# A base product over eight batches at once, with quarters of 512 tokens, in an adapter and LoRA-mixture kernel

## The chip, the cores and the metric

The kernel runs on one core of a Trainium2 chip. The metric is the time of one execution in microseconds as the device reports it, the median of three runs. One further execution was taken with the hardware profiler. TensorE (PE) multiplies matrices and writes to the accumulator memory PSUM, VectorE (DVE) and ScalarE (ACT) work elementwise, and SyncE's queue (SP) issues nearly all transfers. Each engine takes its instructions strictly in the order in which the program lists them, and waits at an instruction until the semaphores that it names have been reached.

## The reference

There are 8 batches of 256 tokens with 1024 features, all in float32. Each batch picks one of eight 1024 x 1024 matrices; its result goes through a base layer with bias, and through a mixture of eight rank-16 LoRA experts whose weights come from a router.

```python
y = einsum('bsi,boi->bso', x, weight[adapter_ids])
base_out = einsum('btd,od->bto', y, base_W) + base_b
probs = softmax(einsum('btd,nd->btn', y, router_W) + router_b)   # 15 outputs
topk_p, topk_i = top_k(probs, 8)
w = einsum('btk,btke->bte', topk_p, onehot(expert_map[topk_i]))
h = einsum('btd,erd->bter', y, A)
lora = einsum('bter,eor->bto', h * w[..., None], B) * 2.0
return x + base_out + lora
```

## The kernel before, in words

**Adapter stage** (lines 284 to 439). One pass of the loop at line 370 handles one batch. It multiplies with seven half-size products in place of eight (Winograd's form): 512 x 512 pieces of the adapter matrix times pieces of x that are 128 tokens wide, in the blocks of `block` (line 238), 16 matmuls each. The results go to `ys[0]` (batches 0 to 3) and `ys[1]` (batches 4 to 7). `project` (line 98) multiplies the batch's y with the stacked A and router matrices into the PSUM tile `ph`; ACT copies the 128 columns of h out of it (line 115), DVE adds the router bias to the other 15 (line 116, tile `lg`), and `weigh` makes the expert weights and the product `hw`. `turn` (line 199) transposes `hw` on PE into `pt` and ACT copies it to `hwTs`. Beside this work `prepare` (line 261) builds, a piece per batch, the seven left operands of the base product, and stores them to a scratch tensor in HBM.

The last batch ends so: blocks for a21, s4 and a22 on PE, then `turn` of batch 6 (line 442), then `project` of batch 7 (line 443). In the DVE queue there stand the add that completes y of batch 7 (line 423), the four differences (`differences`, line 175; instructions on line 186) of the first base product, the eight sums and differences of `prepare(7)` (lines 269 to 276), and then `lg` of batch 7 and its `weigh`.

**Base stage** (lines 449 to 705). It is Winograd's form twice. The outer level has seven products of 512 x 512 pieces of the base matrix and runs once for each of two groups `g` of four batches; each outer product is again seven inner blocks (`product`, line 496). An inner block has four matmuls, stationary 128 x 128 and moving 128 x 256 tokens (`block`, line 474), and in four of seven outer products two more for the LoRA term (line 487). In the trace each float32 matmul is two records. PSUM holds `pa`, `pb` and `pc`, each 2 KB a partition and twice, beside `pe` (line 540) and `pt`. The blocks of one product are, in order, a11 (pa), s1 (pc), s2 (pa), a12 (pb), s3 (pa), s4 (pc), a22 (pa). The value that stands in `pa` is read out (`take`, `plus`) before the next block adds to it, so each block on `pa` waits for the read of the `pa` block before it.

Between the blocks stand the gaps (`gap`, line 530): each puts two waiting DVE steps from the queues `soon` and `later` ahead of the next read. Such steps are differences of inner operands (line 186), outer sums (line 630), and results plus residual x (line 601) with their store. `load_left` (line 163) fetches the left operand of a product, 1 MB and 0.75 MB, two products ahead, once for each group. The last product of all (`split`) has one half of its result in `pe`, so that the first half is added and stored while PE makes the second.

The pools of the base stage are opened after those of the adapter stage are closed (line 449), and lie over the same memory.

Of the kernel before, what the change touches and what calls it, by code (L numbers as in the profile page):

```python
# [28 lines left out]
def kernel(  # L29
# [4 lines left out]
    xr: bass.AP,  # L34
    ids: bass.AP,
# [25 lines left out]
    assert ER == P and E == 8 and B % GB == 0  # L61
# [4 lines left out]

    tpool = ctx.enter_context(tc.tile_pool(name="t", bufs=6))
    ps_t = ctx.enter_context(
        tc.tile_pool(name="ps_t", bufs=1, space=bass.MemoryType.PSUM)
    )  # L70
# [27 lines left out]
    def project(b, ar_sb, rpool, ps_h, order=(0, 1)):  # L98
# [6 lines left out]
        for j in order:  # L105
            for k in range(KC):
                nc.tensor.matmul(  # L107
                    ph[:, j],
                    lhsT=y[:, k // KH, th, k % KH // 2, bi, k % 2, ts(j, P)],
                    rhs=ar_sb[:, k, :],  # L110
                    start=(j == order[0] and k == 0),
                    stop=(k == KC - 1),
                    skip_group_check=True,
                )
# [59 lines left out]

    def differences(right):

        b11, b12, b21, b22 = right[:, 0, 0], right[:, 0, 1], right[:, 1, 0], right[:, 1, 1]
        t = {}

        def minus(n, of, less):  # L180
            def run():
                t[n] = tpool.tile([P, 2 * S], F32, name="tt").rearrange(
                    "p (k o) -> p k o", k=2
                )
                x, y = (t[v] if isinstance(v, int) else v for v in (of, less))
                nc.vector.tensor_sub(t[n], x, y)  # L186
                return t[n]

            return run

        return [minus(1, b12, b11), minus(2, b22, 1), minus(3, b22, b12), minus(4, b21, 2)]


    lefts = [0, 1, 3, 5, 4, 6, 2] * (B // GB)
# [4 lines left out]
    def turn(b, hw):  # L199

        pt = ps_t.tile([P, S], F32, name="pt")
# [5 lines left out]
    with ExitStack() as phase:  # L207
        xpool = phase.enter_context(tc.tile_pool(name="x", bufs=2))
        mpool = phase.enter_context(tc.tile_pool(name="m", bufs=1))
# [7 lines left out]
            tc.tile_pool(name="ps_h", bufs=1, space=bass.MemoryType.PSUM)  # L217
        )
# [151 lines left out]
        for b in range(B):  # L370
            last = b == B - 1

            def out(oh, th):
                return ys[b // GB][:, oh, b % GB // 2, :, b % 2, :, ts(th, P)]
# [18 lines left out]
            if waiting:  # L393
                turn(*waiting)
# [21 lines left out]
            else:  # L416
# [5 lines left out]
                if last:  # L422
                    nc.vector.tensor_add(out(0, 1), pc, u2)
                    left[0] = load_left(lefts[0])
                    terms = [step() for step in differences(ys[0][:, 0, 0])]
                    prepare(b)
                block(pa, q["a22"], t4, False)
                if last:
                    left[1] = load_left(lefts[1])
# [12 lines left out]
        turn(*waiting)  # L442
# [6 lines left out]
    with ExitStack() as phase:  # L449

        mpool = phase.enter_context(tc.tile_pool(name="m2", bufs=1))
        qpool = phase.enter_context(tc.tile_pool(name="q2", bufs=6))
        xpool = phase.enter_context(tc.tile_pool(name="x2", bufs=6))
        vpool = phase.enter_context(tc.tile_pool(name="v", bufs=1))
        ps = phase.enter_context(
            tc.tile_pool(name="ps", bufs=2, space=bass.MemoryType.PSUM)
        )
        ps_e = phase.enter_context(
            tc.tile_pool(name="ps_e", bufs=1, space=bass.MemoryType.PSUM)
# [4 lines left out]
        add, sub = nc.vector.tensor_add, nc.vector.tensor_sub  # L464

# [3 lines left out]
        def fill(n):  # L469
            for _ in range(n):  # L470
                if soon or later:
                    soon.popleft()() if soon else later.popleft()[1]()

        def block(acc, left, right, first, up=None, hw=None):

            for mi in range(2):
                for k in range(2):
                    nc.tensor.matmul(  # L478
                        acc[mi][:, mi, :],
                        lhsT=left[:, 2 * k + mi, :],  # L480
                        rhs=right[:, k, :],
                        start=(first and k == 0 and (mi == 0 or acc[0] is not acc[1])),
                        stop=(up is None and k == 1),
                        skip_group_check=True,
                    )
                if up is not None:
                    nc.tensor.matmul(  # L487
                        acc[mi][:, mi, :],
                        lhsT=up[:, ts(mi, P)],
                        rhs=hw,  # L490
                        start=False,
                        stop=True,
                        skip_group_check=True,
                    )

        def product(left, terms, right, base, into, done, gaps, u=None, hw=None, split=False):
# [6 lines left out]
            b11, b12, b21, b22 = right[:, 0, 0], right[:, 0, 1], right[:, 1, 0], right[:, 1, 1]  # L503
            t1, t2, t3, t4 = terms

            def plus(dst, acc, other):
                if acc[0] is acc[1]:
                    add(dst, acc[0], other)  # L508
                else:
                    for mi in range(2):  # L510
                        add(dst[:, mi], acc[mi][:, mi], other[:, mi])

            def take(dst, acc, i, j):
                if isinstance(base, int):
                    for mi in range(2):
                        c = base + 2 * i + mi
                        nc.scalar.activation(
                            dst[:, mi], acc[mi][:, mi], AF.Identity, bias=bb[:, c : c + 1]
                        )
                else:  # L520
                    plus(dst, acc, base(i, j))

            def term(i, j):
                if u is None:
                    return ()
                if (i, j) == (0, 1):
                    return upd[:, u, :], hw[:, 1, :]
                return up[:, u, i, :], hw[:, j, :]

            def gap(n):  # L530
                for step in gaps.get(n, ()):
                    step()
                fill(2)

            pa = 2 * [ps.tile([P, 2, S], F32, name="pa")]
            pb = 2 * [ps.tile([P, 2, S], F32, name="pb")]
            pc = 2 * [ps.tile([P, 2, S], F32, name="pc")]
            if split:

                pa[1] = ps_e.tile([P, 2, S], F32, name="pe")  # L540
# [4 lines left out]
            gap(1)  # L545
# [5 lines left out]
            gap(3)  # L551
            block(pb, a12, b21, True, *term(0, 0))
            plus(c[0, 0], pb, c[0, 0])
# [3 lines left out]
            plus(c[1, 1], pa, c[1, 1])  # L557
            done(1, 1, c[1, 1])
            gap(5)
            block(pc, s4, b22, False, *term(0, 1))  # L560
            plus(c[0, 1], pc, c[0, 1])
            done(0, 1, c[0, 1])
            gap(6)
            block(pa, a22, t4, False, *term(1, 0))
            take(c[1, 0], pa, 1, 0)

            fill(len(soon))
            while later and later[0][0] not in (c[0, 1], c[1, 0]):
                later.popleft()[1]()
            done(1, 0, c[1, 0])  # L570

        def fresh(i, j):
            return qpool.tile([P, 2, S], F32, name="q")
# [4 lines left out]
        for g in range(B // GB):  # L578
            y, hw = ys[g], hwTs[g]
            end = g == B // GB - 1  # L580
            b11, b12, b21, b22 = y[:, 0, 0], y[:, 0, 1], y[:, 1, 0], y[:, 1, 1]
            u = mpool.tile([P, 2, 2, 2, S], F32, name="u")
            v = vpool.tile([P, 2, 2, 2, S], F32, name="v")
            t2 = mpool.tile([P, 2, 2, 2, S], F32, name="t2")
            xs = {}

            def number(oh, th, i, j):
                return ((g * 2 + oh) * 2 + th) * 4 + 2 * i + j

            def load_x(*r):  # L590
                xs[r] = xpool.tile([P, 2, S], F32, name="xt")
                nc.sync.dma_start(xs[r].rearrange("p m t -> p (m t)"), xr[number(*r)])

            def finish(oh, th):


                def done(i, j, q):
                    x, n = xs[oh, th, i, j], number(oh, th, i, j)

                    def run():  # L600
                        add(q, q, x)  # L601
                        nc.sync.dma_start(outq[n], q.rearrange("p m t -> p (m t)"))

                    later.append((q, run))

                return done

            def joint(i, j, q):


                def run():
                    add(q, v[:, i, j], q)

                soon.append(lambda: add(u[:, i, j], u[:, i, j], q))
                later.append((q, run))
                finish(1, 1)(i, j, q)

            def last(i, j, q):
                if (i, j) == (1, 0):
                    for mi in range(2):  # L620
                        nc.sync.dma_start(outq[number(1, 0, 1, 0), :, ts(mi, S)], q[:, mi])
                else:
                    finish(1, 0)(i, j, q)

            def at(t):
                return lambda i, j: t[:, i, j]

            def update(dst, x, z, quarters=((0, 0), (0, 1), (1, 0), (1, 1))):
                return [
                    (lambda i=i, j=j: sub(dst[:, i, j], x[:, i, j], z[:, i, j]))  # L630
                    for i, j in quarters
                ]

            def first_terms(*quarters):

                for q in quarters:
                    soon.extend(update(b11, b12, b11, [q]))
                    soon.extend(update(t2, b22, b11, [q]))

            seven = [  # L640

                (b11, 0, at(u), nothing),
                (b21, at(u), fresh, finish(0, 0), 0, hw[:, 0]),
                (t2, at(u), at(u), nothing),
                (b11, at(u), at(v), nothing, 1, hw[:, 1]),
# [131 lines left out]
```

## Time and profile before

| what | us |
|---|---|
| median of 3 runs (lowest to highest) | 443.89 (443.81 to 443.92) |
| the profiled execution's own time | 442.66 |
| its span, first to last instruction | 440.9 |
| adapter stage, to the first base matmul | 240.16 |
| base stage on PE, to the end of the last matmul's stream | 197.46 (240.16 to 437.62) |
| from there to the end of the span | 3.3 |

The profiled execution took 1.76 us more than its span, and 1.23 us less than the median. Durations below come from it. A row of the timeline gives a start, the time from the first start to the last end, the engine, the line, what is written from what, and how many instructions are merged. Records of PE overlap: one is 0.38 us long, but the next begins well before it ends, so a matmul costs the distance of two starts and not the length of a record. The same holds in part for DVE.

### The profile page before, as it was taken

What the parts mean: (1) busy time and instruction counts of PE and PEld (TensorE: products, weight loads), DVE (VectorE), ACT (ScalarE), POOL (GpSimd) and SP (SyncE); (2) the same over time, 40 slices, a digit from 0 to 9 for tenths busy, and PEclk for the clock granted to TensorE, in tenths of its full rate; (3) what the DMA queues carried; (4) which work ended last, traced back from release to release, by engine and by line L of the source; (5) the groups of instructions that cost most, each with busy time, mean ns of one, the idle gap of its engine ahead of it and who ended that gap; (6) DMA issues with size and microseconds to landing.
All of it is one profiled execution on the core that took longest, in us unless ns stands there. A gap on an engine that the chain in (4) does not pass through costs nothing.

```text
span 440.9 us, 7299 instructions
## 1 busy us (share of the span) xinstructions
PE 434.5 (99%) x2994; PEld 409.7 (93%) x2994; DVE 303.2 (69%) x516; ACT 40.4 (9%) x89; POOL 0.7 (0%) x6
## 2 busy tenths in 40 slices
PE   7999999999999999999999999999999999999997
PEld 6999999999999999999999888888888888888886
DVE  2579695682963967939629957755597858755594
ACT  1101111011011110110111200000200200000200
POOL 0000000000000000000000000000000000000000
PEclk9999999999999999999999999999999999999999
DMA  8989879678597797893370956821967726921843
GB/s 303 407 348 349 313 273 273 219 282 308 181 284 274 240 290 266 266 315 143 134 297 0 371 226 238 337 115 37 354 249 261 277 89 214 371 83 53 306 153 133
DMA packets 34050, 106.19 MB, mean 241 GB/s; under 512 B 3298, under 2 KB 7138, under 8 KB 30818
## 3 DMA queue, kind: packets, MB, share of 16 engines
q1 hardware_dynamic: 33730, 104.69, 67.0%
q10 hardware_dynamic: 288, 1.05, 0.6%
q8 instruction: 23, 0.38, 0.3%
q14 instruction: 9, 0.07, 0.0%
HBM read 84.49 MB, written 21.23 MB: 240 GB/s over the span
## 4 chain that ended last, share of the span: by engine, by line
PE 92%; DVE 5%; DMA 1%; issue 1%; SPq 0%
PE pa L243 24%; PE pa L478 20%; PE pc L243 12%; PE pc L478 10%; PE pb L243 7%; PE ph L107 6%; PE pb L478 5%; PE pc L487 3%; PE pb L487 2%; PE pa L487 1%; DMA wt<-in_w_dram 1%; DVE tt L186 1%; PE pe L478 1%; DVE y L630 0%; PE pt L203 0%
## 5 line engine op out<-in xcount | busy, mean ns | idle before, releaser
L478 PE MATMUL pa<-tt,wt 128*128 128x256 f32 x324 | 78.0, 379 | 0.1
L478 PEld LDWEIGHTS pa<-tt,wt 128*128 128x128 f32 x324 | 61.4, 190 | 8.9 <-DVE u L508 0.5
L243 PE MATMUL pa<-x,wt 128*128 128x128 f32 x512 | 59.9, 275 | 1.8 <-DMA wt<-in_w_dram 1.8
L243 PEld LDWEIGHTS pa<-x,wt 128*128 128x128 f32 x512 | 58.5, 192 | 2.2 <-issue 1.3
L243 PE MATMUL pa<-tt,wt 128*128 128x128 f32 x480 | 56.0, 275 | 0.0
L243 PEld LDWEIGHTS pa<-tt,wt 128*128 128x128 f32 x480 | 54.8, 192 | 0.0
L116 DVE TENSOR_TENSOR lg<-ph,rb 128x30 f32<-128x30 f32 x8 | 1.5, 189 | 49.9 <-ACT h L115 49.9
L107 PE MATMUL ph<-ar_sb,y 128*128 128x143 f32 x256 | 32.7, 284 | 0.0
L107 PEld LDWEIGHTS ph<-ar_sb,y 128*128 128x128 f32 x256 | 31.8, 190 | 0.0
L243 PE MATMUL pc<-tt,wt 128*128 128x128 f32 x256 | 29.9, 275 | 0.0
L243 PE MATMUL pc<-x,wt 128*128 128x128 f32 x256 | 29.9, 275 | 0.0
L243 PE MATMUL pb<-x,wt 128*128 128x128 f32 x256 | 29.9, 275 | 0.0
L243 PEld LDWEIGHTS pc<-tt,wt 128*128 128x128 f32 x256 | 29.2, 192 | 0.0
L243 PEld LDWEIGHTS pc<-x,wt 128*128 128x128 f32 x256 | 29.2, 192 | 0.0
L243 PEld LDWEIGHTS pb<-x,wt 128*128 128x128 f32 x256 | 29.2, 192 | 0.0
L478 PE MATMUL pc<-tt,wt 128*128 128x256 f32 x112 | 27.8, 379 | 0.0
L342 DVE TENSOR_TENSOR wt<-wt 128x2048 f32<-128x2048 f32 (+1 forms) x9 | 18.5, 2051 | 10.2 <-DMA wt<-in_wq_dram 10.2
L478 PE MATMUL pc<-y,wt 128*128 128x256 f32 x96 | 24.0, 379 | 0.0
L478 PE MATMUL pb<-y,wt 128*128 128x256 f32 x96 | 24.0, 379 | 0.0
L478 PEld LDWEIGHTS pc<-tt,wt 128*128 128x128 f32 x112 | 21.2, 190 | 3.0
L478 PE MATMUL pa<-y,wt 128*128 128x256 f32 x92 | 21.9, 379 | 0.0
L601 DVE TENSOR_TENSOR q<-q,xt 128x512 f32<-128x512 f32 x31 | 21.3, 686 | 0.5
(117 smaller groups left out, 488.0 us busy)
## 6 DMA issues: line engine op xcount, KB each, us to landing
wt<-in_wq_dram SPq DMA_DIRECT2D x21, 1024.0 KB, 6.1
wt<-left_raw SPq DMA_DIRECT2D x14, 1024.0 KB, 5.5
wt<-left_sum SPq DMA_DIRECT2D x14, 768.0 KB, 8.0
xt<-in_xr_dram SPq DMA_DIRECT2D x32, 256.0 KB, 6.8
out_dram<-q SPq DMA_DIRECT2D x31, 256.0 KB, 2.3
x<-in_xq_dram SPq DMA_DIRECT2D x7, 1024.0 KB, 4.9
wt<-in_w_dram SPq DMA_DIRECT2D x16, 256.0 KB, 2.8
wt<-in_w_dram SPq DMA_DIRECT2D x8, 512.0 KB, 4.9
```

The lines of the kernel that those rows point to most:

```text
L107: nc.tensor.matmul(ph[:, j], lhsT=y[:, k // KH, th, k % KH // 2, bi, k % 2, ts(j, P)], rhs=ar_sb[:, k, :], start=(j == order[0] and k == 0 ...
L116: nc.vector.tensor_add(lg, ph[:, :, ER:], rb.unsqueeze(1).to_broadcast([P, NTT, N]))
L186: nc.vector.tensor_sub(t[n], x, y)
L243: nc.tensor.matmul(acc[:, m // 2, m % 2, :], lhsT=left[:, k, ts(m, P)], rhs=right[:, k, :], start=(first and n == 0), stop=(k == KH - 1), ...
L342: nc.vector.tensor_add(q["s1"][:, h], q["a21"][:, h], q["a22"][:, h])
L478: nc.tensor.matmul(acc[mi][:, mi, :], lhsT=left[:, 2 * k + mi, :], rhs=right[:, k, :], start=(first and k == 0 and (mi == 0 or acc[0] is n ...
L487: nc.tensor.matmul(acc[mi][:, mi, :], lhsT=up[:, ts(mi, P)], rhs=hw, start=False, stop=True, skip_group_check=True,)
L601: add(q, q, x)
```

## The change

- The base stage no longer runs twice. One outer pass handles all eight batches: quarters are now 512 tokens wide (`W = 2 * S`), `b11` and `b21` come from batches 0 to 3 and `b12` and `b22` from batches 4 to 7. A matmul moves 128 x 512.
- Each of the seven left operands is loaded once, in gap 0 of the product before (`left.update`), into slots that the product two before has just left.
- `pa` has two buffers, `pb` and `pc` have one, and each is 4 KB a partition. The pools `ps_t`, `ps_h` and `ps` of the adapter stage are all closed ahead of them; batch 7's transpose uses a buffer of `pa`.
- The differences `t1` to `t4` live in two tiles of the weight pool. Of the first product's, `t1` and `t2` stand before `prepare(7)` on DVE, `t3` and `t4` after it.
- The outer sums are made in place in `y`, as lists of steps of 1024 columns; the order of the outer products is 0, 1, 3, 4, 6, 5, 2. The bias enters with the first product on ACT, and for the other half with `scalar_tensor_tensor` on DVE.
- Result tiles (`q`) are four, x tiles three, both twice as large; each x load is asked for when a result is stored.
- The last block is issued as 128 x 512 for the first half and 2 x (128 x 256) for the second, with three adds and three stores behind it (`end`).

In the instruction order that the changed kernel builds to, the DVE queue from the last add into y of batch 7 on reads: t1, t2, the eight steps of `prepare(7)`, t3, t4, then `lg` of batch 7 and the rest of its routing without a break, then four differences and four outer sums before the first read of a PSUM block. The first base matmul waits for the left operand and for the add that makes that `lg`; before, it waited for its left operand and for work of PE alone. The first of the three adds at the end waits for the last matmul.

```diff
 def differences(right):
-    b11, b12, b21, b22 = right[:, 0, 0], right[:, 0, 1], right[:, 1, 0], right[:, 1, 1]
+    b11, b12, b21, b22 = (quarter(right, i, j) for i in range(2) for j in range(2))
...
-                t[n] = tpool.tile([P, 2 * S], F32, name="tt").rearrange(
-                    "p (k o) -> p k o", k=2
-                )
+                if n % 2:
+                    t["two"] = wpool.tile([P, KH, OH], F32, name="wt")
+                t[n] = t["two"][:, ts((n - 1) % 2, 2)]
...
-    lefts = [0, 1, 3, 5, 4, 6, 2] * (B // GB)
+    lefts = [0, 1, 3, 4, 6, 5, 2]
...
                 if last:
                     nc.vector.tensor_add(out(0, 1), pc, u2)
                     left[0] = load_left(lefts[0])
-                    terms = [step() for step in differences(ys[0][:, 0, 0])]
+                    steps = differences(ys[0][:, 0])
+                    terms = [step() for step in steps[:2]]
                     prepare(b)
                 block(pa, q["a22"], t4, False)
                 if last:
-                    left[1] = load_left(lefts[1])
+                    terms += [step() for step in steps[2:]]
...
-        ps = phase.enter_context(
-            tc.tile_pool(name="ps", bufs=2, space=bass.MemoryType.PSUM)
-        )
-        ps_e = phase.enter_context(
-            tc.tile_pool(name="ps_e", bufs=1, space=bass.MemoryType.PSUM)
+        ps_b = phase.enter_context(
+            tc.tile_pool(name="ps_b", bufs=1, space=bass.MemoryType.PSUM)
+        )
+        ps_a = phase.enter_context(
+            tc.tile_pool(name="ps_a", bufs=2, space=bass.MemoryType.PSUM)
         )
...
+        W = 2 * S
...
-            pa = 2 * [ps.tile([P, 2, S], F32, name="pa")]
-            pb = 2 * [ps.tile([P, 2, S], F32, name="pb")]
-            pc = 2 * [ps.tile([P, 2, S], F32, name="pc")]
+            pa = ps_a.tile([P, 2, W], F32, name="pa")
+            pb = ps_b.tile([P, 2, W], F32, name="pb")
+            pc = ps_b.tile([P, 2, W], F32, name="pc")
...
+            if end is not None:
+                fill(len(soon) + len(later))
+                block(pa, a22, t4, False, *term(1, 0), (1, 2))
+                end(pa)
+                return
...
+        def end(pa):
+            dst = u[:, 1, 0]
+            for mi, cut in ((0, ds(0, W)), (1, ds(0, S)), (1, ds(S, S))):
+                add(dst[:, mi, cut], pa[:, mi, cut], dst[:, mi, cut])
+                nc.sync.dma_start(
+                    outq[number(1, 0, 1, 0)].rearrange("p (m t) -> p m t", m=2)[:, mi, cut],
+                    dst[:, mi, cut],
+                )
...
+        b11, b12, b21, b22 = ys[0][:, 0], ys[1][:, 0], ys[0][:, 1], ys[1][:, 1]
+        seven = [
+            (b11, None, 0, at(u), nothing),
+            (b21, at(u), None, fresh, finish(0, 0), 0, hw1),
+            (b12, at(u), None, at(u), nothing),
+            (b22, at(u), None, at(v), nothing, 2, hw2),
+            (b11, at(u), KH, at(u), nothing),
+            (b12, None, None, fresh, joint, 1, hw2),
+            (b21, at(u), None, at(u), finish(1, 0), 1, hw1),
+        ]
+        sums = {
+            0: update(b12, sub, b22, b12) + update(b12, add, b12, b11),
+            2: update(b11, sub, b12, b11),
+            3: update(b21, sub, b21, b12) + update(b12, sub, b22, b12),
+        }
...
+            if not last:
+                gaps[0].append(lambda m=n + 1: left.update({m: load_left(lefts[m])}))
...
+                gaps[0].append(lambda o=steps + sums.get(n, []): soon.extend(o))
```

## The prediction

> **What bounds the kernel now.** I read the busy shares first, then the chain of work that ended last, then the list of waits for PE alone, then the timeline at the two places where the stages meet and end.
>
> ```profile
> span 440.9 us, 7299 instructions
> PE 434.5 (99%) x2994; PEld 409.7 (93%) x2994; DVE 303.2 (69%) x516; ACT 40.4 (9%) x89; POOL 0.7 (0%) x6
> PE 92%; DVE 5%; DMA 1%; issue 1%; SPq 0%
> ```
>
> PE is never free and the chain runs through it. The list of waits for PE has two entries in the whole span:
>
> ```profile
> PE pa L243 <- DMA wt<-in_w_dram: 1.8, 2, 1.1
> PE pt L365 <- POOL ident masks.py:199: 1.4, 1, 1.4
> ```
>
> Both lie in the first 9 us, which the change doesn't touch. So the time is the adapter stage (to 240.16 us), PE's stream in the base stage (197.46 us), and what follows its end. A change pays only by fewer or shorter matmuls, and costs by any pause of PE that it makes.
>
> What a base matmul costs is read from starts, in a timeline of PE alone:
>
> ```profile
> 101.19 3.74 PE L243 MATMUL pa<-tt,wt 128*128 128x128 f32 x32
> ...
> 311.57 1.89 PE L478 MATMUL pa<-y,wt 128*128 128x256 f32 x8
> 313.30 1.89 PE L478 MATMUL pc<-tt,wt 128*128 128x256 f32 x8
> 315.02 1.89 PE L478 MATMUL pa<-tt,wt 128*128 128x256 f32 x8
> ```
>
> Eight records of 256 columns take (315.02 - 311.57)/2 = 1.726 us, 215.8 ns each; the 32 records of 128 columns from 101.19 to the next row's start at 104.76 take 111.6 ns each. The base stage has 14 products x 7 blocks x 4 matmuls x 2 records = 784, and 8 LoRA products x 4 blocks x 2 x 2 = 128 more: 912 x 0.2158 = 196.8 us, plus one transpose pair, 0.44 us: 197.25 of the 197.46 us. No bubble is there to be won.
>
> **The matmuls.** The count of columns stays: 7 x 7 x 4 x 2 = 392 and 4 x 4 x 2 x 2 = 64, 456 records of 512 columns, of which 6 in the last block are issued as 12 of 256. No row has 512 columns, so I bound it. Doubling the row gives 431.6 ns; then nothing changes (0.0). The line through the rows of 128 and 256 columns gives 215.8 + 2 x 104.2 = 424.2, and 450 x 0.4242 + 12 x 0.2158 + 0.44 = 193.9 us, -3.3. The Trainium skill (TensorE: Matmul & The Clock Gate, "Wait — 56ns, not 53.3ns?") says that a warm matmul costs its columns at the array clock and a fixed 2.5 ns. With that, of the 215.8 ns some 213.3 are columns, and 512 take 2 x 213.3 + 2.5 = 429.1 ns (an estimate from that page and the row): 195.7 + 0.44 = 196.1 us, **-1.1 us**. I take the page's, since the 128-column row carries more per record (111.6 - 106.65 = 4.9 ns) than a fixed 2.5 explains, which makes the line too steep.
>
> **Where the stages meet.** This is the part that decides. The timeline of all engines there:
>
> ```profile
> 232.64 0.69 DVE L423 TENSOR_TENSOR y<-pc,u 128x512 f32<-128x512 f32 x1
> 233.25 0.68 DVE L186 TENSOR_TENSOR tt<-y 128x512 f32<-128x512 f32 x1
> ...
> 236.23 4.09 PE L107 MATMUL ph<-ar_sb,y 128*128 128x143 f32 x32
> ...
> 240.16 1.89 PE L478 MATMUL pa<-y,wt 128*128 128x256 f32 x8
> ...
> 240.41 0.37 ACT L115 COPY h<-ph 128x256 f32<-128x256 f32 x1 [3.34 <-PE ph L107]
> ...
> 242.17 0.18 DVE L116 TENSOR_TENSOR lg<-ph,rb 128x30 f32<-128x30 f32 x1
> ```
>
> PE goes from `project` of batch 7 straight into the base stage at 240.16. DVE is behind: it reaches `lg` of that batch 2 us later, and nobody minds. In the changed order the first base matmul waits for this very `lg`: as built, the pool of `pa` covers the place of `ph`, and its first tile waits for `ph`'s last reader (before, only `pe` lay there, first used in the last product). So PE's queue stands behind DVE's, and with it everything.
>
> When does `lg` come? DVE steps of 512 columns start 0.60 us apart, or 0.72 where one needs the one before (233.25 to 233.97 in the timeline). For 1024 columns one row exists:
>
> ```profile
> L342 DVE TENSOR_TENSOR wt<-wt 128x1024 f32<-128x1024 f32 x2 | 2.5, 1226 | 7.5 <-DMA wt<-in_wq_dram 7.4
> ```
>
> 1226 against 686 ns is 0.54 more, so 1.14 us apart, 1.26 for a dependent one. From 233.25, as in the trace: t1 1.26 (t2 needs it), t2 1.14, `prepare(7)` five dependent steps 0.72 and three at 0.60 = 5.4, t3 and t4 2 x 1.14: 10.1 us, `lg` at 243.35, done at 243.54. PE starts at 243.6 and not at 240.16: **+3.4 us**. Ends: 3.2 if the dependent steps run at 0.69, 3.7 if the semaphore and the first weight load add 0.3.
>
> Does the late DVE cost more behind that? `lg` to the end of `weigh` takes 3.9 us (0.7 to the exponential, 0.3 on ACT, 2.9 from the sum to `hw`, as 229.68 to 232.64 in batch 6): 247.3. Four differences to 251.9, four outer sums to 256.5. A block without LoRA is 8 x 0.4291 = 3.43 us, so from 243.6 block a12 ends at 257.3, s3 at 260.8, s4 at 264.2. DVE reads a12 at 257.5, does two sums to 261.0, reads s3 to 262.2. Block a22 needs that read and may start at 264.2: 2 us to spare. (Had PE started at 240.16, a22 would want to start at 260.8; DVE, no longer held up by PE, would be done with that read at 261.2: 0.4 us.)
>
> In products 1 to 6 a block on `pa` needs the read of the block two before it. In the densest, product 2, DVE gets per block two steps and one read, 3 x 1.14 = 3.42 us against 3.43; followed by hand from 299.0, the read of s2 ends at 310.7 and block s3 needs it at 312.7. With LoRA a block is 5.15 us, so DVE gains. In product 6 the reads stand behind residual adds that wait for x; the second read ends near 423, needed at 426. I find no second wait: 0, at worst 2 to 3 us.
>
> **Transfers.** Seven fetches of 1.75 MB fall away (14 to 7 in the list of issues); that is 12.3 MB off queues that delay PE nowhere past 9 us, so worth 0. The new fetch is asked for one product ahead, when the slots of the product before come free, behind stores on SP's queue that wait for DVE. Its medians to landing are 5.5 and 8.0 us; a product lasts 24.0 or 30.9 us. That cover hides it; if the stores held SP for 15 us longer, PE would wait. ACT's reads of 1024 columns (two of 512, near 0.59 each by the copies on lines 392 to 406) have a whole block of 3.43 us: 0. DVE's total barely moves (some 206 steps of 512 columns become about 100 of 1024 and a few small ones).
>
> **The end.**
>
> ```profile
> 437.10 1.51 SPq L621 DMA_DIRECT2D out_dram<-q  x2
> 437.19 0.59 PE L487 MATMUL pe<-hwT,up 128*128 128x256 f32 x2
> 437.82 0.42 DVE L511 TENSOR_TENSOR q<-pe,u 128x256 f32<-128x256 f32 x1 [0.84 <-PE pe L487]
> ```
>
> Now one add of 256 columns stands between the last matmul and the last store: 0.42 us. With the change all three adds wait for the last matmul: 0.60 + 0.34 + 0.42 = 1.36 us (512 columns 0.60 apart, 256 columns 0.34 as on line 511). **+0.95**; ends +0.6, if the last store was not what ended last, and +1.5, if 256 KB more in front of it cost half a microsecond.
>
> **Sum.** +3.4 - 1.1 + 0.95 = +3.2 on the profiled 442.66: 445.9. The median stands 1.23 above that execution, so **447.1 us**. Own range: 443.89 + 3.2 - 3.3 + 0.6 = 444.4 to 443.89 + 3.7 + 0 + 1.5 = 449.1.
>
> **Rivals.**
>
> - *The clock drops in the pause* (0.13). The same page ("The HAM clock gate") says that an idle window of about 3.4 us halves PE's clock until about 3.4 us of work have passed, and it warns against pauses of that length: it speaks against this change. In the trace the slices of the granted clock show full speed throughout, but its longest pauses are 1.4 and 1.1 us, so no row here tells. By the rows, 447.1; by the rule, if tripped, 3.4 to 6.8 us of half speed cost 1.7 to 3.4 more: 448.8 to 450.5. My pause is 3.4, just at the edge, and a free-running window fits into it rarely.
> - *DVE or x arrives late further on* (0.08): reads in products 2 and 6 have 2 to 3 us to spare. A transfer 4 us late gives 448 to 450. Against it: PE waits for neither in the whole base stage today.
> - *Moving 512 gains nothing* (0.12), the records behaving as two of 256: 431.6 ns, 448.2 us.
> - *Faster* (0.05), one mechanism: PE is not held at 240.16, because `lg` gets in before the bulk of DVE's steps, and wide matmuls are as cheap as the steep line. Then -3.3 + 0.95 and the 0.4 at block a22 give 441.9 us (with 429.1 ns 444.1). For it: today nothing on DVE holds PE there, and the line comes from two rows. Against it: DVE's order is fixed, and 10 us of steps stand before `lg`. With 424.2 ns it decides from a pause below 2.3 us; with 429.1 ns, from one below 0.15.
>
> The forecast itself has 0.62. A measurement of this kernel can't tell less than about 0.2% (0.9 us) from no change. Faster by more 0.04, within it 0.04 (a short pause or cheap matmuls), slower 0.92. The range for 8 in 10 takes in the own range and most of the clock's case: 444.4 to 450.0.
>
> **What would show it.** Right: a PE pause near 3.4 us before the first 512-column matmul, released by DVE's `lg`; blocks 3.43 us apart; no PE wait above 0.5 us behind it; three DVE adds after the last matmul; granted clock full. Wrong: the base stage starting at 240.2; a record pitch of 424 or 432 ns; PE waiting for DVE inside products 2 or 6; a granted clock below 1 after 243 us.

## The result, and the profile after

| | before | changed |
|---|---|---|
| median of 6 runs (lowest to highest), us | 443.78 (443.41 to 443.92) | 448.65 (447.7 to 449.88) |
| ratio, 95% interval | | 1.0115 (1.0103 to 1.0127) |
| profiled execution, us | 442.66 | 448.5 |
| its span, us | 440.9 | 446.7 |
| first base matmul begins, us | 240.16 | 244.68 |
| last matmul's stream ends, us | 437.62 | 441.83 |

The change makes the kernel 1.15% slower: 4.9 us by the medians, 5.84 by the two profiled executions. The first part of the page after:

```profile
span 446.7 us, 6139 instructions
PE 434.8 (97%) x2544; PEld 325.5 (73%) x2544; DVE 298.7 (67%) x413; ACT 36.3 (8%) x69; POOL 0.7 (0%) x6
```

PE is as busy in microseconds as before (434.8 against 434.5), in a span that is 5.8 us longer: nearly all of what was lost is idle PE. The list of waits for PE after (total, times, longest) names two that did not exist before, for `lg` and for `u`:

```profile
PE pa L486 <- DVE lg L112: 3.3, 1, 3.3
...
PE pa L486 <- DVE u L519: 0.8, 1, 0.8
```

**Where the stages meet.** The timeline of all engines after (start, duration, engine, line, out<-in, count, idle before and its releaser):

```profile
234.35 1.21 DVE L186 TENSOR_TENSOR wt<-y 128x1024 f32<-128x1024 f32 x1
...
237.34 4.09 PE L103 MATMUL ph<-ar_sb,y 128*128 128x143 f32 x32
...
243.31 1.22 DVE L186 TENSOR_TENSOR wt<-y,wt 128x1024 f32<-128x1024 f32 x1
...
244.45 0.18 DVE L112 TENSOR_TENSOR lg<-ph,rb 128x30 f32<-128x30 f32 x1
...
244.68 3.70 PE L486 MATMUL pa<-y,wt 128*128 128x512 f32 x8 [3.26 <-DVE lg L112]
```

The last row is the first base matmul, and its bracket says that it was idle until `lg`. From t1 (234.35) to `lg` (244.45) DVE has work without a gap, 10.1 us. The place where PE would have gone on is found from the `ph` row: before, the base stage began 3.93 us after it (236.23 to 240.16), so here 241.26. The pause is 244.68 - 241.26 = 3.42 us.

**The stream.** PE alone, two blocks without LoRA after:

```profile
303.37 3.60 PE L486 MATMUL pc<-wt 128*128 128x512 f32 x8
306.81 3.60 PE L486 MATMUL pa<-wt 128*128 128x512 f32 x8
```

Starts 3.43 to 3.44 us apart for 8 records: 429.1 ns each over several blocks. The whole stream takes 197.15 us, 0.31 less than before. By the pitches (450 records at 429.1 ns and 12 at 215.8, against 912 at 215.8) it should be 1.1 less; the wait for `u` in the last product, 0.84, takes the rest back. All engines there:

```profile
423.04 1.22 DVE L619 TENSOR_TENSOR q<-q,xt 128x1024 f32<-128x1024 f32 x1 [3.22 <-DMA xt<-in_xr_dram]
...
425.57 1.23 DVE L619 TENSOR_TENSOR v<-v,xt 128x1024 f32<-128x1024 f32 x1 [1.31 <-DMA xt<-in_xr_dram]
...
426.71 1.22 DVE L519 TENSOR_TENSOR u<-pa,u 128x1024 f32<-128x1024 f32 x1
...
427.98 3.70 PE L486 MATMUL pa<-wt 128*128 128x512 f32 x8 [0.84 <-DVE u L519]
```

The read on line 519 had its data since about 422 (block s2 was through). It stands in DVE's queue behind two adds of x, and both wait for their x to land.

**The end.** The last rows of the same timeline:

```profile
441.40 0.59 PE L495 MATMUL pa<-hwT,up 128*128 128x256 f32 x2
442.03 1.35 DVE L638 TENSOR_TENSOR u<-pa,u 128x512 f32<-128x512 f32 x3 [2.68 <-PE pa L495]
442.75 1.30 SPq L639 DMA_DIRECT2D out_dram<-u  x3
```

Three adds in 1.35 us follow the last matmul, where one of 0.42 did before: +0.93. From the end of the last add (443.38) to the end of the span go 3.36 us against 2.66: +0.70. Together +1.63.

The profiled difference: pause 3.42, stream -0.31, end 1.63, and 1.10 that arose ahead of all this: the `ph` row lies at 237.34 against 236.23. That last part isn't the change's. Other profiles with the same adapter stage have that row at 236.20, 236.30 and 236.37 (e5_busy, e10_best, e9_order), others at 237.0 to 237.5. Two things in the first 12 us of an execution move it: how the first weights arrive (waits of 0.6 to 2.4 us for `in_w_dram`), and how far apart the first records stand. In a0_again the wait is only 0.6 us and the row is late all the same (237.30): the 32 records of its first block (6.17 to 11.79) take 5.62 us in place of 3.57, as if a part of them ran at half clock, though the clock row reads 1.00 there.

### The profile page after: what moved, and what is told of

It is laid out like the page before. It is cut to its first block, busy times and chain, and to the rows that moved or that the text cites. A ratio compares the mean times of both kernels' runs of the same rounds, so it can differ in the third digit from the quotient of the medians.

```text
span 446.7 us, 6139 instructions
## 1 busy us (share of the span) xinstructions
PE 434.8 (97%) x2544; PEld 325.5 (73%) x2544; DVE 298.7 (67%) x413; ACT 36.3 (8%) x69; POOL 0.7 (0%) x6
## 4 chain that ended last, share of the span: by engine, by line
PE 89%; DVE 5%; DMA 3%; issue 1%; SPq 0%; ACT 0%; DVEq 0%
PE pa L246 24%; PE pa L486 20%; PE pc L246 12%; PE pc L486 10%; PE pb L246 7%; PE ph L103 6%; PE pb L486 5%; PE pc L495 3%; DMA xt<-in_xr_dram 2%; PE pa L495 2%; DMA wt<-in_w_dram 1%; PE pb L495 1%; DVE v L619 1%; DVE wt L186 1%; DVE u L519 1%
## 5 line engine op out<-in xcount | busy, mean ns | idle before, releaser
L486 PE MATMUL pa<-wt 128*128 128x512 f32 (+1 forms) x172 | 76.5, 583 | 0.8 <-DVE u L519 0.8
L486 PEld LDWEIGHTS pa<-wt 128*128 128x128 f32 x172 | 32.5, 190 | 40.6 <-issue 38.5
L246 PEld LDWEIGHTS pa<-tt,wt 128*128 128x128 f32 x480 | 54.8, 192 | 0.0
L246 PEld LDWEIGHTS pc<-tt,wt 128*128 128x128 f32 x256 | 29.2, 192 | 0.0
L486 PE MATMUL pa<-y,wt 128*128 128x512 f32 x56 | 25.3, 594 | 3.3 <-DVE lg L112 3.3
L486 PE MATMUL pc<-wt 128*128 128x512 f32 x56 | 25.8, 592 | 0.0
L486 PE MATMUL pc<-y,wt 128*128 128x512 f32 x56 | 25.8, 592 | 0.0
L486 PE MATMUL pb<-y,wt 128*128 128x512 f32 x56 | 25.8, 592 | 0.0
L486 PEld LDWEIGHTS pa<-y,wt 128*128 128x128 f32 x56 | 10.6, 190 | 16.4 <-issue 12.9
L486 PEld LDWEIGHTS pb<-y,wt 128*128 128x128 f32 x56 | 10.6, 190 | 13.4 <-issue 13.4
```

The source lines that it names most:

```text
L246: nc.tensor.matmul(acc[:, m // 2, m % 2, :], lhsT=left[:, k, ts(m, P)], rhs=right[:, k, :], start=(first and n == 0), stop=(k == KH - 1), ...
L486: nc.tensor.matmul(acc[:, mi, at], lhsT=left[:, 2 * k + mi, :], rhs=right[:, k, at], start=(first and k == 0), stop=(up is None and k == 1 ...
```

## The experiments

Each kernel was timed in five rounds beside the kernel before. Kernels measured at different times are compared by their ratios to it; 0.001 is 0.44 us.

| kernel | median, us | ratio, 95% interval |
|---|---|---|
| a0_again, the changed kernel | 450.0 | 1.0135 (1.0103 to 1.0168) |
| e1_swap, pools in the other order | 444.75 | 1.0018 (1.0006 to 1.003) |
| e2_lg_first, t3 and t4 behind `weigh` | 445.54 | 1.0034 (1.0021 to 1.0048) |
| e3_twice, t3 three times | 452.83 | 1.0204 (1.0179 to 1.0229) |
| e5_busy, PE busy in the pause | 447.35 | 1.0091 (1.0075 to 1.0107) |
| e11_half, PE busy in half of it | 447.33 | 1.0084 (1.0071 to 1.0097) |
| e6_pieces, e1_swap in 256 columns | 445.3 | 1.0038 (1.0025 to 1.0051) |
| e7_x_early, e1_swap, four x earlier | 447.79 | 1.0087 (1.0065 to 1.0109) |
| e8_all, e7_x_early, last sum in two tiles | 445.54 | 1.0038 (1.0025 to 1.0051) |
| e9_order, e1_swap, read ahead of x | 444.75 | 1.0023 (1.0014 to 1.0033) |
| e10_best, e9_order, last sum in two tiles | 443.45 | 0.9991 (0.9982 to 1.0001) |
| e12_split, e1_swap, last sum in two tiles | 443.69 | 1.0004 (0.9996 to 1.0012) |

### The changed kernel once more: a0_again

No edit.

> The changed kernel once more, for a second profile and its spread. Theory P (PE is held at the start of the base stage until DVE has made lg): again a pause of 3.3 us before the first base matmul, ended by lg, and a median of 448 to 449.5 us. Theory C (part of the loss is a lower clock after the pause): some executions show a granted clock below full in the 10 us after the pause. Theory X (x loads of the last product come late): a wait of PE for a DVE read in the last product again, between 0 and 2 us, and different from the 0.8 us seen first, which would go with the spread of 2.2 us between runs.

The ratio agrees with the first within the intervals. The profile shows something that the first does not. PE alone:

```profile
244.65 5.40 PE L486 MATMUL pa<-y,wt 128*128 128x512 f32 x8 [3.26 <-DVE lg L112]
249.88 3.60 PE L486 MATMUL pc<-wt 128*128 128x512 f32 x8
```

The pause is the same 3.26 us, but the first block takes 249.88 - 244.65 = 5.23 us, not 3.54. The stretches of 1 us (length; busy time of PE, of PEld, its weight loads, of DVE, ACT and POOL, with the number of instructions; then the granted clock, DMA share, GB/s):

```profile
245.00:246.00 1.00, 1.00 (x3) 0.38 (x2) 0.58 (x4) 0.23 (x1) 0.00 (x0) 0.92 1.02 374
246.00:247.00 1.00, 1.00 (x2) 0.33 (x1) 0.90 (x9) 0.00 (x0) 0.00 (x0) 0.50 1.02 313
...
248.00:249.00 1.00, 1.00 (x3) 0.48 (x2) 0.98 (x2) 0.00 (x0) 0.00 (x0) 0.50 0.95 355
249.00:250.00 1.00, 1.00 (x3) 0.43 (x3) 0.97 (x2) 0.00 (x0) 0.00 (x0) 0.87 1.02 434
```

The clock was halved for 0.16 + 3 + 0.26 = 3.42 us, after the pause was over: a loss of 1.7 us that no list of waits shows, since PE counts as busy. In the first profile of the changed kernel the clock stayed at 1.00 through the same microseconds. So the loss comes in some executions and not in others. This is a rival that the prediction named, and it had to be measured.

### Taking the pause away: e1_swap, e2_lg_first

e1_swap opens the pools in the other order, so that `pa` no longer covers the place of `ph`:

```diff
-        ps_b = phase.enter_context(
-            tc.tile_pool(name="ps_b", bufs=1, space=bass.MemoryType.PSUM)
-        )
         ps_a = phase.enter_context(
             tc.tile_pool(name="ps_a", bufs=2, space=bass.MemoryType.PSUM)
         )
+        ps_b = phase.enter_context(
+            tc.tile_pool(name="ps_b", bufs=1, space=bass.MemoryType.PSUM)
+        )
```

> The two PSUM pools of the base stage are opened in the other order, so that pb and pc, and not pa, lie over the place of ph; nothing else. The wait for lg is then put on pc, 3.4 us later in PE's order. Theory P: no pause before the first base matmul, under 0.3 us before the second block, some 0.4 us before block a22 of the first product (its read comes behind the same DVE steps), so about -2.9: 445.7 us. Theory X or the width of the matmuls as the main cause: less than 1 us gained, 448 or more.

e2_lg_first leaves the pools and shortens the queue before `lg`:

```diff
                 block(pa, q["a22"], t4, False)
-                if last:
-                    terms += [step() for step in steps[2:]]
...
         waiting = B - 1, weigh(nh, nex, route, rpool, const)
+        terms += [step() for step in steps[2:]]
```

> The differences t3 and t4 of the first base product stand behind batch 7's routing on DVE and not before its lg; the wait of the first matmul stays. Theory P: lg comes 2.28 us earlier (two steps of 1.14), the pause is 3.3 - 2.3 = 1.0 us, the time about 446.4. Rivals: no change above 0.5 us.

Of the waits for PE in e1_swap only these lie behind the first 12 us:

```profile
PE pa L486 <- DVE u L519: 0.9, 1, 0.9
PE pa L486 <- DVE u L560: 0.2, 1, 0.2
```

The wait for `lg` is gone: the `ph` row starts at 236.25 and the base stage at 240.18, 3.93 us behind it as in the kernel before, and the clock is 1.00 there. In e2_lg_first's profile the wait for `lg` is 1.0 us and the clock is full until the last matmul. Both took more off than the pause alone: e1_swap 0.0117 against a0_again on the same chip, 5.2 us, where 3.4 us of pause less the forecast 0.4 at block a22 make about 3; e2_lg_first 4.5 us, where two steps of 1.14 make 2.3. The surplus is about 2 us in both, and about 1.3 against the first measurement of the changed kernel (1.0115); a half-clock stretch of 1.7 us is of that size. That the pause sits where the prediction put it, and comes from the order of two pool openings, is shown.

### A longer pause: e3_twice

t3 is made two more times ahead of `lg`.

```diff
                     terms += [step() for step in steps[2:]]
+                    for _ in range(2):
+                        nc.vector.tensor_sub(
+                            terms[2],
+                            quarter(ys[0][:, 0], 1, 1),
+                            quarter(ys[0][:, 0], 0, 1),
+                        )
```

> The difference t3 is made two more times before lg (same result): the suspected cost is lengthened by 2.3 to 2.5 us. Theory P: the pause grows one for one, to 5.6 to 5.8 us, and the time to about 451.0. Theory C: a pause that long drops the granted clock for 3.4 us or more behind it, 1.7 to 3.4 us more, 452.6 to 454.5, and the clock row shows it. If the pause were covered by later slack, the time would stay at 448.7.

452.83 lies in the range of the clock's theory. PE alone in e3_twice:

```profile
246.86 6.37 PE L492 MATMUL pa<-y,wt 128*128 128x512 f32 x8 [5.67 <-DVE lg L112]
253.07 3.60 PE L492 MATMUL pc<-wt 128*128 128x512 f32 x8
```

The wait is 2.4 us longer, as two steps make it, and the first block takes 6.21 us, 2.67 over 3.54. The clock is halved from 245.44 to 252.26 by the stretches of 1 us, 6.82 us: twice as long as in a0_again. It fell while PE still stood idle, so 5.4 of these 6.82 us held work, which makes the 2.7 lost. All six runs have a mean granted clock of 0.989 to 0.993; a0_again has 0.990 to 0.998.

### PE kept busy in the pause: e5_busy and e11_half

The direct test. Identity products fill the pause, into a bank that nothing reads; the base stage begins when it did.

```diff
         nh, nex = project(B - 1, ar_sb, rpool, ps_h, (1, 0))
+        idle = ps_t.tile([P, S], F32, name="pt")
+        for _ in range(15):
+            nc.tensor.matmul(idle[:, :P], lhsT=ident, rhs=ident, start=True, stop=True)
```

> The changed kernel with one thing more: between batch 7's weigh matmuls and the first base matmul TensorE does 15 identity products of 128 columns (30 records of 111.6 ns, 3.35 us by the row of such products), which fill the pause of 3.3 us, write to a bank that nothing reads, and end before lg lets the base product begin. The place of the base product stays (about 244.7 in the profile). Theory 'clock': in most executions the pause is followed by some 3.5 us at half the granted clock (the second profile of the changed kernel: 0.50 from 246 to 249, first block of 8 records 5.4 us instead of 3.7), about 1.75 us a time; with TensorE busy this goes: 450.0 and 448.65 become about 447.6 (447.2 to 448.3), no half clock between 244 and 253, mean granted clock 0.997 or more in every run, a narrower spread. Rival 'only the pause': the clock's share is in no median, 448.6 to 450.0 as before. If the extra products come into the base stage's way: later than 450.

e11_half has 7 of them in place of 15.

> As e5_busy, but with 7 identity products in the pause instead of 15: they cover 1.6 of the 3.4 us and leave TensorE idle for about 1.8 us before the first base matmul, which begins when it did. If only a pause of more than 1.8 us halves the clock: as e5_busy, ratio 1.009, no half clock after the pause, mean clock 0.997 or more in most runs. If a pause of 1.8 us halves it too: ratio 1.0115 to 1.0135 as with the whole pause, first 8 records near 5.4 us, mean clock 0.995.

PE alone in e5_busy:

```profile
236.20 4.09 PE L103 MATMUL ph<-ar_sb,y 128*128 128x143 f32 x32
240.13 3.51 PE L450 MATMUL pt<-ident 128*128 128x128 f32 x30
243.69 3.70 PE L489 MATMUL pa<-y,wt 128*128 128x512 f32 x8
247.23 3.60 PE L489 MATMUL pc<-wt 128*128 128x512 f32 x8
```

The base stage begins 7.49 us after the `ph` row, where the changed kernel has 7.34: the pause is as long as ever for the product, only filled. The first block takes 3.54 us. And the kernel is faster: 1.0091 against 1.0115 and 1.0135. Work that nobody needs took 1.1 to 2.0 us off, the clock's share of the median. The mean clock is 0.997 or more in five of the six runs, not in all as forecast (0.996 in the slowest, 449.21 us). In e11_half:

```profile
240.93 1.72 PE L450 MATMUL pt<-ident 128*128 128x128 f32 x14
244.41 3.67 PE L489 MATMUL pa<-y,wt 128*128 128x512 f32 x8 [1.76 <-issue]
```

An idle stretch of 1.8 us is left, the clock doesn't fall (first block 3.51 us; means of 0.998 to 1.000 in all five runs), and the ratio is that of e5_busy. The interval of e5_busy (to 1.0107) just overlaps those of the changed kernel (from 1.0103), that of e11_half (to 1.0097) does not. From these two to e1_swap, 0.0066 to 0.0073 or about 3 us, is the pause itself. So the theory of a bare pause falls: it is about 3 us of pause and 1 to 2 us of clock behind it.

### What the wide matmuls gain: e6_pieces

```diff
-        def block(acc, left, right, first, up=None, hw=None, pieces=(1, 1)):
+        def block(acc, left, right, first, up=None, hw=None, pieces=(2, 2)):
...
-                            start=(first and k == 0),
+                            start=(first and k == 0 and n == 0),
```

> The kernel of e1_swap (444.75) with each base matmul of 512 columns issued as two of 256, nothing else changed. If each record costs 2.5 ns beside its columns, as the two pitches say (215.8 at 256, 429.1 at 512), 456 records more cost 456 x 2.5 = 1.1 us: 445.9, pitch 215.8. If the gain at 512 came from elsewhere (fewer left loads): 444.75 unchanged with a pitch of 214.6.

PE alone in e6_pieces:

```profile
310.81 3.62 PE L486 MATMUL pa<-wt 128*128 128x256 f32 x16
314.27 3.62 PE L486 MATMUL pc<-y,wt 128*128 128x256 f32 x16
```

Sixteen records take 3.455 us (300.45 to 314.27 is four such blocks), against 3.433 for the eight of 512: 215.9 and 429.1 ns, so 2.7 ns more for each record that is added, on the same columns and with the same operands. That a record has a fixed cost is shown by the profile. The ratio rose by 0.0020, 0.9 us of the 1.1 expected, but the two intervals overlap, so the times alone would not show it.

### The wait for x: e7_x_early, e9_order

e7_x_early asks for four x at the start of the last product, into two free weight tiles:

```diff
+        def ask_four():
+            for _ in range(2):
+                two = wpool.tile([P, KH, OH], F32, name="wt")
+                for n in range(2):
+                    r = wanted.pop()
+                    xs[r] = two[:, ts(n, 2)]
+                    nc.sync.dma_start(
+                        xs[r].rearrange("p m t -> p (m t)"), xr[number(*r)]
+                    )
...
+                gaps[0].append(ask_four)
```

> The kernel of e1_swap (444.75) with the last four x tiles of the outer sum asked for at the start of the last product, into two weight tiles that are free by then, instead of one at a time behind the stores. Theory 'x is late': TensorE's wait of 0.9 us for the add before the last product's block s3 goes, 444.75 - 0.9 = 443.85; DVE's waits for x of 3 us near 420 go from the profile. Rival 'x is hidden, DVE itself is late': 444.75, the same wait. If the earlier transfers hold the right operands up: over 445.

Later than 445, though it isn't the right operands that are held up. DVE alone in e7_x_early:

```profile
421.86 1.22 DVE L629 TENSOR_TENSOR q<-q,xt 128x1024 f32<-128x1024 f32 x1 [5.06 <-DMA xt<-in_xr_dram]
424.36 1.23 DVE L629 TENSOR_TENSOR v<-v,xt 128x1024 f32<-128x1024 f32 x1 [1.28 <-DMA xt<-in_xr_dram]
425.50 1.22 DVE L519 TENSOR_TENSOR u<-pa,u 128x1024 f32<-128x1024 f32 x1
```

The four early transfers, 2 MB, are issued ahead of the x that is needed first; it lands later (a wait of 5.06 us, against 3.29 in e1_swap), and PE's wait for `u` grew from 0.9 to 2.7 us. The ratio rose by 3.1 us, more than these 1.8; three of the six runs have a mean clock of 0.993 to 0.996, so the longer wait seems to have halved the clock in them, which the profiled run doesn't show. e9_order asks for nothing earlier and moves the read ahead of the adds instead:

```diff
-            gap(2)
+            if end is None:
+                gap(2)
             block(pa, s2, t2, False)
             take(c[0, 1], pa, 0, 1)
+            if end is not None:
+                gap(2)
```

> The kernel of e1_swap (444.75, ratio 1.0018) with one edit in the last product: the two adds of x that gap 2 places ahead of the read of block s2 are placed behind it, so the read that TensorE waits for no longer stands behind an x that is still on its way. Nothing is asked for earlier (e7_x_early did that, and delayed the x that was needed first: wait 2.7 us in place of 0.9). Theory 'the read stands behind x': no wait of TensorE near block s3 of the last product, ratio 1.0018 - 0.9/444 = 0.9998, about 443.7. Rival 'the x that is moved blocks a later read as long': the wait turns up at block a22 of the last product (add of L560), 444.7.

In its profile PE's wait for `u` on line 519 is gone, and none of its size stands in its place: the 0.2 us that the list still names are at block a22 of the first product, as in e1_swap. The median did not move: 1.0023 against 1.0018. The edit does what it says in the profile, and its worth in the median isn't shown by this pair.

### The end: e8_all, e10_best, e12_split

The last product's sum gets two tiles, so that the add of the first half has to wait only for the first half's matmuls; other reads of `pa` there become two (`plus`).

```diff
-            pa = ps_a.tile([P, 2, W], F32, name="pa")
+            pa = 2 * [ps_a.tile([P, 2, W], F32, name="pa")]
+            if end is not None:
+                pa[1] = ps_a.tile([P, 2, W], F32, name="pa")
...
-                add(dst[:, mi, cut], pa[:, mi, cut], dst[:, mi, cut])
+                add(dst[:, mi, cut], pa[mi][:, mi, cut], dst[:, mi, cut])
```

> The changed kernel with three edits together: pools in the other order (no pause), x early, and the last product's sum in two tiles, so that the adds of the first half wait for the first half's matmuls alone. Sum: 444.75 - 0.9 (x) - 0.6 (tail: the two adds of the first half leave the end, of three in 1.35 us) = 443.25, against 443.8 for the kernel before: 0.1% faster than it. If the tail is set by the last store's landing alone, 443.85; if x was hidden, 444.15; if both, 444.75.

e8_all has e7_x_early's edit in it and took over its fault (PE's wait for `u` was 2.3 us); it stayed slower than before. The other two leave that edit out:

> e9_order with the last product's sum in two tiles, so that the add of the first half waits only for the first half's matmuls. In e8_all one split add lay beside the last matmuls and two short ones (0.76 us) stood behind them, against three (1.35 us) before: 0.6 us less at the end than e9_order, ratio about 0.9985, 443.1. If the end is set by the stores' landing alone: as e9_order.

> e10_best without the edit of e9_order: pools in the other order and the last product's sum in two tiles, the adds of x before the read of block s2 as in the changed kernel. It tells what each of the two edits is worth, since e1_swap to e10_best (both edits) gave 1.0018 to 0.9991, 1.2 us, but e9_order alone gave nothing (1.0023). If the wait for x costs 0.9 us in every execution: TensorE waits 0.5 to 0.9 us for the read of s2 again and the ratio is 0.9991 + 0.0020 = 1.0011. If the wait costs the median nothing and the end is all: ratio 0.9991 as e10_best.

DVE alone at the end of e10_best:

```profile
435.18 0.69 DVE L655 TENSOR_TENSOR u<-pa,u 128x512 f32<-128x512 f32 x1
436.89 0.76 DVE L655 TENSOR_TENSOR u<-pa,u 128x256 f32<-128x256 f32 x2 [1.03 <-PE pa L495]
```

The wide add lies beside the last matmuls, and only 0.76 us stand behind them. By the ratios, e12_split is 0.0014 below e1_swap, 0.6 us, which is what was put on the split; e10_best has 0.9991 where 0.9985 was forecast. e12_split's 1.0004 lies between its own two forecasts (1.0011 if the wait for x costs 0.9 us in every execution, 0.9991 if it costs nothing). Between e12_split and e10_best, e9_order's edit is worth 0.0013, 0.6 us; between e1_swap and e9_order it was worth -0.0005. The intervals are too wide to choose, and what that wait costs in the median, between nothing and 0.9 us, stays open.

e10_best is the best version found. Its interval includes 1: the base product over all batches, rid of what it had cost, can't be told from the kernel before.

## Why the prediction was right, and where it was off

The direction, the place and the main mechanism were right. The measured 448.65 lies in the stated range, with help from its width: the forecast of 447.1 was 1.5 us short, the repeated 450.0 lies on the range's edge, and one of the prediction's own signs of being wrong, a granted clock below 1 after 243 us, came in the second profile. Step by step:

- **What bounds it.** Right: every loss came from PE standing idle, running at half clock, or from what lies behind its last matmul.
- **Stage meeting, +3.4 us.** Right in mechanism and size. From t1 to `lg` 10.1 us were forecast and 10.10 measured; the pause was 3.42. e1_swap shows the cause: with the two pools in the other order it is gone.
- **Matmuls, -1.1 us.** Right. 429.1 ns had been worked out from the row of 256 columns and the fixed 2.5 ns of the Trainium skill (TensorE: Matmul & The Clock Gate, "Wait — 56ns, not 53.3ns?"), and 429.1 was measured; the line through the rows of 128 and 256 columns (424.2) was wrong, as the text argued, but in the other sense: with 104.2 ns for 128 columns more it is too flat, not too steep (256 to 512 columns cost 213.3, or 106.65 for 128). e6_pieces measures 2.7 ns a record.
- **The end, +0.95.** The adds are +0.93, as forecast. The last stores took 0.70 us more to land, which the forecast had at 0 and only its upper end (+1.5) allowed for; +1.63 in all is just over that. It is no accident of one execution: every profile with this end has 4.9 us from the last matmul to the end of the span, where the kernel before has 3.3.
- **"I find no second wait: 0, at worst 2 to 3 us."** This step failed. It read the second read of product 6 as ending near 423, needed at 426; it ended at 427.9, and 0.8 us of PE was lost in the first profile, 0.5 to 0.9 in five others and nothing in three. The mechanism was named (reads behind residual adds that wait for x), but no landing of x was worked out, while an x of 512 KB took 5.2 us to land at the median and is asked for only when a store before it is issued.
- **Rival "the clock drops in the pause", 0.13, 448.8 to 450.5.** Under-weighted, and this is the main miss. The forecast held the full clock to be likelier, since a free-running window would fit into a pause of 3.4 us rarely. It need not fit in: about 2.2 us of idle PE in a window were enough (last section). The mean granted clock agrees. That mean also holds the fall behind the last matmul, which costs nothing, but that takes off 0.003 at most (e5_busy's profile: 0.997, with full clock up to the last matmul). So a run at 0.996 or less had a half-clock stretch elsewhere: 10 of the 12 runs of the changed kernel, and 3 of the 50 in which that pause is gone, shortened or filled (e1_swap, e2_lg_first, e5_busy, e11_half). A stretch of 3.42 us lowers the mean of a 447 us span by 0.5 x 3.42 / 447 = 0.004, which is what lies between the twelve (0.9946) and the five of e11_half (0.9988). That the first profile had none was chance. The share of the median, 1.1 to 2.0 us (e5_busy against the two), is what the rival had put at 1.7.
- **The median.** Forecast 447.1, measured 448.65 (450.0 when repeated). From 443.8: pause 3 and clock 1 to 2 by the experiments; end 1.6, x up to 0.9, and the matmuls -1.1. e1_swap shows the last three together: +0.8 us.

Of the other rivals, "512 gains nothing" falls with the pitch, and "faster" with the pause. Nothing was lost by the left operands: PE waits for none of them in any list of waits here.

## What to carry to other kernels

Where one stage's memory is laid over another's, look up who reads last in the place that the pool of the next stage's first tile takes, and where that read stands in its engine's queue. The tile itself need not lie there: as built, the first `pa` takes banks 4 and 5 of PSUM and `ph` lay in bank 6, which is in the pool's other buffer. The order of two pool openings was worth 1.0 to 1.2% here. Count a pause of TensorE of 2.4 to 5.7 us, the lengths seen here, at more than its length, since a stretch at half clock can follow that no wait shows: compare the length of the first blocks behind it, and the mean clock of many runs, not one profile. A transfer asked for earlier delayed the one that was needed first (e7_x_early), so try first to move the urgent instruction ahead of the waiting one.

## What the runs showed of the hardware

- **The granted clock falls in steps of one length.** Halved stretches lasted 3.42 us (a0_again), 3.40 (e8_all) and 6.82 (e3_twice), near one and two of the 3.4 us that the Trainium skill (TensorE: Matmul & The Clock Gate, "The HAM clock gate") gives for a free-running window of activity. In a0_again and e8_all it began after PE was at work again. That the window runs on by itself can be read here: in a0_again the clock fell at 245.84 and, behind the last matmul, at 447.23, which is 201.39 us or 59 x 3.4133 later; in e3_twice at 245.44 and 450.24, 60 x 3.4133; in e8_all at 427.18 and 447.66, 6 x 3.4133.
- **A pause shorter than that is enough.** PE alone in e8_all:

```profile
423.26 1.02 PE L495 MATMUL pb<-hwT,up 128*128 128x512 f32 x2
426.56 5.40 PE L486 MATMUL pa<-wt 128*128 128x512 f32 x8 [2.28 <-DVE u L519]
```

The two records end at 424.12, so PE was idle for 2.4 us, and yet the block behind it ran at half clock (5.23 us to the next at 431.79). The same section has the clock fall after at least one idle window of about 3.4 us; here the measurement decides.

- **What counts is the idle time in one window.** In every profile the clock falls at least once, at the latest behind the last matmul, up to 1.5 us past the end of the span. For the first profile of the changed kernel:

```profile
444.00:445.00 1.00, 0.00 (x0) 0.00 (x0) 0.00 (x0) 0.00 (x0) 0.00 (x0) 0.68 0.99 350
```

0.64 us of this stretch are at half clock, so a window ended at 444.36. Steps of 3.4133 us back from such a fall give the windows of that execution, and the rows of PE how long it was idle in each:

| how the window ended | us of idle PE in it |
|---|---|
| the clock fell | 2.20 (e5_busy, behind the last matmul), 2.22 (a0_again, in the pause), 2.44 (e8_all, above), 2.47 and 2.52 (behind the last matmul in e10_best and in the first profile), 3.28 or more in all others |
| it did not fall | among others 1.69 and 1.72 (the pause of the first profile, cut in two by a boundary near 242.96), 1.14 and 1.67 (the wait of 2.8 us in e7_x_early), 1.11 and 0.81 (e11_half), 2.08 and 2.14 (behind the last matmul in e9_order and e8_all) |

So in these 14 profiles the clock fell when PE had been idle for 2.20 or more of a window's 3.41 us, and did not fall at 2.14 or less. This fits without exception, but it was found after the runs, and no run was made to test it. The clock came back after a window of unbroken work (a0_again, e8_all), and not after one with 1.42 us of idle PE (e3_twice, which so had two halved windows). An estimate from these figures: a pause of 3.42 us is spared when a boundary falls 1.2 to 2.2 us into it, 1.0 of 3.41 us, so in three executions of ten. Two of the twelve runs of the changed kernel show a mean clock as if spared.
